# Flamingo stack on one core: layer 2's first group ahead of layer 1's last down products, and three tiles' softmax weights on two engines

## The chip, the cores and the metric

The kernel runs on one core of a Trainium2 chip as one launch. The metric is the device time of a run in microseconds (us), lower is better. A core has five engines that work side by side, each through its own queue in order: TensorE (PE in the profile, with PEld for its weight loads), VectorE (DVE), ScalarE (ACT), GpSimd (POOL) and SyncE (SP, which here only issues DMAs). Three timed runs of the kernel before took 826.50, 824.56 and 826.20 us, median 826.2 us.

## The reference, cut to what matters

The input x has 4 sequences of 256 tokens, each 256 wide: 1024 tokens. Eight steps follow each other, each adding a gated residual:

```python
x = x + tanh(g_xattn[0]) * L0_xattn(layernorm(x), ctx)   # latent attention, 16 heads, 64 context rows
x = x + tanh(g_ffn[0])   * L0_ffn(layernorm(x))          # 16 experts, top 6
x = x + tanh(g_xattn[1]) * L1_xattn(layernorm(x), ctx)   # latent attention without rope on the queries
x = x + tanh(g_ffn[1])   * L1_ffn(layernorm(x))          # ternary weights, 256 -> 1024 -> 256, gelu
x = x + tanh(g_xattn[2]) * L2_xattn(layernorm(x), ctx)   # 16 heads of 16, causal mask
x = x + tanh(g_ffn[2])   * L2_ffn(layernorm(x))          # int8 linear
x = x + tanh(g_xattn[3]) * L3_xattn(layernorm(x), ctx)
x = x + tanh(g_ffn[3])   * L3_ffn(layernorm(x))          # 8 experts, top 2
```

Each attention takes `softmax(scores)` over 64 context rows for each of 16 heads: per token 16 groups of 64 numbers, each group less its maximum, through exp, and divided by its sum. `layernorm` takes mean and variance over the 256 columns of a token. The change concerns the end of `L1_ffn` (its second product, here called the down product), the start of `L2_xattn`, and the division by the sum in `L0_xattn` and `L1_xattn`.

## The kernel before, in words

The 1024 tokens are 8 tiles of 128 (`NT = 8`), in two groups of 4 (`NG = 2`, `TPG = 4`). x stays on chip; tile t is `x[t]`, 128 x 256.

All four attentions run through `in_flight` (L519), a loop of 11 steps written out by hand. Step i does, in this order: one step of a generator `beside` (other work that is laid between); `scores(i)`: products into a PSUM tile "wide", then maximum (`mx`), subtraction and exp into the tile `attn`; `gated_add(i - 3)`, which adds the finished tile to x (L517); `weights(i - 1)` (L486); and `attend(i - 2)`. There are two buffers of "wide", so scores(i) can start only when the subtraction of tile i - 2 has read its buffer, and four PSUM buffers "mm" for nearly everything else.

`weights` (L486) adds up each of the 16 groups of 64 (L490, VectorE), inverts the sums (L491, VectorE) and multiplies the whole 128 x 1024 tile `attn` by them in place on GpSimd (L492). `attend` begins with `transposed_pairs` (L498): eight 128 x 128 transposes on TensorE (L506) in two halves of four, each half copied out by ScalarE (L507) into `attnT`. The first half reads the first 512 columns of `attn` (heads 0 to 7), the second half the rest. In layers 0 and 1 (`latent_attend`, L677) eight products follow (L714). In layers 2 and 3 (`attention23`, L1037) come eight small products (L1109), a ScalarE copy (L1118) and the output product (L1121).

`attention23` has its own `queries(g)` for a group of 4 tiles: `layernorm(g)` (statistics L430 and L433 on VectorE, a square root L435 on ScalarE, a reciprocal L438 and four normalisations L449 on VectorE), `transposed` (L461, copies L169 or L171), and `head_queries` (L1028: eight products L476, and two ScalarE multiplications L1034). Group 0 of layer 2 is made beforehand, inside `ffn1` (L1886), and handed over as `kept[2, 0]`; group 1 is the generator's first three steps, so it lies at steps 0, 1 and 2 of `in_flight`, beside steps of `keys_values` for layer 3.

`ffn1` ends with the eight down products `down(g, i)` (L1916): 24 products of 128 x 256 in bf16 (L1920), an addition of the bias (L1928) and a gated addition (L517). Between those of group 1 it lays the steps of `keys_values(2, ...)` (L987: a memset, two key products L1000 with VectorE writes L1007, and four value products L1016 with copies), `layernorm(0)`, `transposed(xn)` and `head_queries(2, ...)`. After them, `used("L1_w2")` frees a weight slot, so that the next load (`w_L_sgu`) is issued, and `load_experts3` (L325) issues the loads of four experts of layer 3, two DMAs each, into the space that held the hidden activations.

The order of instructions on each engine is set by a scheduler when the program is built: it takes what is ready by its own estimate of times, and among what is ready the earlier in the program's text. `side_by_side` (L150) raises the priority of all but the first product of the scores.

Of the kernel before, what the change touches and what calls it, by code (L numbers as in the profile page):

```python
# [97 lines left out]
def tile_flamingo(ctx: ExitStack, tc: tile.TileContext, a: dict, out: bass.AP):  # L98
# [212 lines left out]
    def used(name):  # L311

        del loaded[name]
        at[1] += 1
        issue()
# [167 lines left out]
        nc.vector.tensor_tensor(e, src, mx.unsqueeze(2).to_broadcast([P, groups, n]), ALU.subtract)  # L483
        nc.scalar.activation(e, e, AF.Exp)  # L484

    def weights(e):  # L486

        groups, n = e.shape[1], e.shape[2]
        sm = sb.tile([P, 16], F32, tag="sm", name="sm", bufs=3)[:, :groups]
        nc.vector.tensor_reduce(sm, e, AX.X, ALU.add)  # L490
        nc.vector.reciprocal(sm, sm)  # L491
        nc.gpsimd.tensor_tensor(e, e, sm.unsqueeze(2).to_broadcast([P, groups, n]), ALU.mult)  # L492

    def softmax_inplace(e, src):
        exponentials(e, src)
# [20 lines left out]
    def gated_add(t, ps, gate):  # L516
        return nc.vector.scalar_tensor_tensor(x[t], ps, gate, x[t], ALU.mult, ALU.add)  # L517

    def in_flight(scores, attend, gate, beside=iter(())):  # L519

        made, outs = {}, {}
        for i in range(NT + 3):
            next(beside, None)
            if i < NT:
                made[i] = scores(i)
            if i >= 3:
                gated_add(i - 3, outs.pop(i - 3)[:, :D], gate)
            if 1 <= i <= NT:
                weights(made[i - 1])
            if 2 <= i < NT + 2:  # L530
                outs[i - 2] = attend(i - 2, made.pop(i - 2))

# [144 lines left out]
    def latent_attend(products, wvo, gate, swapped=False, beside=iter(())):  # L677


        vos: dict = {}  # L680

        def values(b):

            v = region(("wqk", "weff")[b % 2], 2048, "vo").rearrange("p (q j o) -> p q j o", q=4, j=2)
            for r in range(2):
                pss = [ps_mm() for _ in range(2)]
                for a_ in range(2):
                    for j, ps in enumerate(pss):
                        rows = slice(j * DC, (j + 1) * DC)
                        nc.tensor.matmul(  # L690
                            ps[a_ * L : (a_ + 1) * L, :],
                            bd_k[rows, b, j * L : (j + 1) * L],
                            wvo[rows, 4 * r + a_ : 4 * r + a_ + 3 : 2, :],
                            start=True,
                            stop=True,
                        )
                for j, ps in enumerate(pss):
                    evacuate(v[:, 2 * r : 2 * r + 2, (1 - j) if swapped and b >= B // 2 else j, :], ps.rearrange("p (q o) -> p q o", q=2))
            vos[b] = v.rearrange("p q j o -> p (q j) o")

        def scores(t):
            if t % 2 == 0:
                values(t // 2)
            ps = ps_wide()
            products(ps, t)
            e = t4([P, NH, L], "attn")
            exponentials(e, ps.rearrange("p a (h l) -> p (a h) l", l=L))
            return e

        def attend(t, e):  # L710
            aT, vo = transposed_pairs(e), vos[t // 2]
            ps = ps_mm()
            for s in range(NP):
                nc.tensor.matmul(ps[:, :D], aT[:, s, :], vo[:, s, :], start=(s == 0), stop=(s == NP - 1))  # L714
            return ps

        in_flight(scores, attend, gate, beside)

    def attention0(gate):

# [316 lines left out]
    def attention23(layer, gate, beside):  # L1037
        kbd, vbd = kept.pop(layer)
        w = loaded[f"L{layer}"]
        w_o = w[:, 512:1024].rearrange("p (c o) -> p c o", c=2)  # L1040
        qT = []

        def queries(g):

            xn = layernorm(g, layer == 3)
            yield
            xT = transposed(xn)
            yield
            qT.append(head_queries(layer, xT))

        if (layer, 0) in kept:
            qT.append(kept.pop((layer, 0)))
        else:
            for _ in queries(0):
                pass

        def scores(t):


            g, i = divmod(t, TPG)  # L1060
            ps = ps_wide()
            masked = t % 2 == 0
            if masked:
                for a in range(2):
                    nc.tensor.matmul(
                        ps[:, a, :].rearrange("p (h l) -> p h l", l=L),
                        ident16,
                        causal16.unsqueeze(1).to_broadcast([P, 8, L]),
                        start=True,
                        stop=False,  # L1070
                    )

            def part(half, a):
                rows = slice(a * L, (a + 1) * L)
                return nc.tensor.matmul(
                    ps[:, a, half * D : (half + 1) * D],
                    qT[g][rows, half, i * P : (i + 1) * P],
                    kbd[rows, half, t // 2].rearrange("p i l -> p (i l)"),
                    start=not masked,
                    stop=(half == 1 or not masked),  # L1080
                )

            last = side_by_side(lambda half=half, a=a: part(half, a) for half in range(2) for a in range(2))
            if layer == 3 and t == 2:
                kept_busy(1, ps_mm(), last)

            e = t4([P, NH, L], "attn")
            src = ps.rearrange("p a (h l) -> p (a h) l", l=L)
            mx = small([P, NH], "mx")
            nc.vector.tensor_reduce(mx, src, AX.X, ALU.max)  # L1090
            for a in range(2):
                nc.vector.tensor_tensor(
                    e.rearrange("p (f a i) l -> p a f i l", f=2, a=2)[:, a],
                    ps[:, a, :].rearrange("p (f i l) -> p f i l", f=2, l=L),
                    mx[:, a * 8 : (a + 1) * 8]
                    .rearrange("p (f i) -> p f i", f=2)
                    .unsqueeze(3)
                    .to_broadcast([P, 2, 4, L]),
                    ALU.subtract,
                )  # L1100
            nc.scalar.activation(e, e, AF.Exp)
            return e

        def attend(t, e):
            aT = transposed_pairs(e)
            ps = ps_mm()
            for pr in range(NP):
                half, r = divmod(pr, 4)
                nc.tensor.matmul(  # L1109
                    ps[r * 32 : (r + 1) * 32, half * P : (half + 1) * P],  # L1110
                    vbd[:, t // 2, pr].rearrange("p j d -> p (j d)"),
                    aT[:, pr, :],
                    start=True,
                    stop=True,
                    tile_position=(0, r * 32),
                )
            cT = sb.tile([P, 2 * P], F32, tag="xn", name="ctxTok", bufs=AHEAD + 2)
            nc.scalar.copy(cT, ps[:, : 2 * P])  # L1118
            ps = ps_mm()
            for half in range(2):  # L1120
                nc.tensor.matmul(  # L1121
                    ps[:, :D], cT[:, half * P : (half + 1) * P], w_o[:, half, :], start=(half == 0), stop=(half == 1)
                )
            return ps

        in_flight(scores, attend, gate, zip_longest(queries(1), beside))
        if layer == 3:
            used("L3")

# [756 lines left out]
    def ffn1(gate):  # L1886
# [29 lines left out]
        def down(g, i, terms):  # L1916
            ps = ps_mm()
            for f in range(8):
                for k in range(3):
                    nc.tensor.matmul(  # L1920
                        ps[:, :D],
                        terms[:, k, f, i * P : (i + 1) * P],
                        w2[:, f, :],
                        start=(f == 0 and k == 0),
                        stop=(f == 7 and k == 2),
                    )
            y = sb.tile([P, D], F32, tag="xn", name="y", bufs=AHEAD + 2)
            nc.vector.tensor_tensor(y, ps[:, :D], b2_1, ALU.add)  # L1928
            gated_add(g * TPG + i, y, gate)

        terms = [up(g) for g in range(NG)]
        used("L1_w1")
        for i in range(TPG):
# [1 line left out]
        kept["values"] = values = region("wqk", 2048, "values")  # L1935
        keys = keys_values(2, region("weff", 2048, "kbd2"), values[:, :1024])
        next(keys)
        down(1, 0, terms[1])
        next(keys)
        xn = layernorm(0)  # L1940
        down(1, 1, terms[1])
        next(keys)
        down(1, 2, terms[1])
        for _ in range(2):
            next(keys)
        down(1, 3, terms[1])
        xT_2 = transposed(xn)
        for _ in keys:
            pass
        kept[2, 0] = head_queries(2, xT_2)  # L1950
        used("L1_w2")
        load_experts3(EARLY3, E3)


    def quantised():
# [240 lines left out]
```

## Time and profile before

One execution was profiled. Its own time was 824.72 us, its span (first to last instruction) 822.9 us; so 1.8 us lie around the span.

| | busy us | share of the span | instructions |
|---|---|---|---|
| PE (matmuls) | 776.0 | 94% | 4507 |
| PEld (weight loads) | 520.6 | 63% | 4510 |
| DVE | 497.2 | 60% | 1146 |
| ACT | 291.7 | 35% | 508 |
| POOL | 246.0 | 30% | 211 |

| stage | us from the span's start |
|---|---|
| layer 0 attention, its tiles in flight | 142.7 to 204 |
| layer 0 experts | 204 to 395 |
| layer 1 attention, its tiles in flight | 408 to 483 |
| layer 1 FFN | 483 to 530 |
| layer 2 attention, its tiles in flight | 535 to 584.5 |
| layer 2 FFN | 584.5 to 599 |

In a timeline a row gives start, length, engine, line, operation, output and inputs, how many such instructions the row merges, and in brackets how long the engine stood idle before it and which instruction ended that. "L492" is line 492 of the kernel.

### The profile page before, as it was taken

The numbers are of one execution on the slowest core, as the hardware profiler recorded it, in microseconds if no ns is written. First come the engines' busy times: TensorE is split into PE (matmuls) and PEld (weight loads), VectorE is DVE, ScalarE is ACT, GpSimd is POOL, SyncE is SP. The second block draws the span as 40 slices with busy tenths as digits, with TensorE's granted clock in tenths as the row PEclk, the third lists the DMA queues.
The fourth block names the chain that finished last, engine by engine and source line by source line (L and its number), as shares of the span: only waits on it lengthen the run. The fifth ranks groups of instructions, "written<-read, shape, count | busy, mean of one in ns | idle before, by whom it ended". The sixth has DMA issues, their size and how long they took to land. (4 is left out here: it accounts for less than half of the span.)

```text
span 822.9 us, 12507 instructions
## 1 busy us (share of the span) xinstructions
PE 776.0 (94%) x4507; PEld 520.6 (63%) x4510; DVE 497.2 (60%) x1146; ACT 291.7 (35%) x508; POOL 246.0 (30%) x211
## 2 busy tenths in 40 slices
PE   6999999898999999999999999998798899999994
PEld 5544433787564776766556566755445647999993
DVE  5565455874693455534878759888769564334331
ACT  3121112343421333422543568166455421233320
POOL 1355444322123344222021110024424103444332
PEclk9999999999999999999999999999999999999998
DMA  9510115800121253333930001630000102232211
GB/s 358 181 39 0 58 39 190 281 18 11 30 63 50 68 130 73 64 74 81 336 111 1 8 1 33 229 129 1 26 1 2 52 9 78 54 50 42 29 16 18
DMA packets 32467, 62.44 MB, mean 76 GB/s; under 512 B 5552, under 2 KB 19504, under 8 KB 31696
## 3 DMA queue, kind: packets, MB, share of 16 engines
q1 hardware_dynamic: 25008, 51.91, 18.3%
q0 software_dynamic: 7104, 9.41, 6.9%
q8 instruction: 39, 0.64, 0.3%
q10 hardware_dynamic: 288, 0.26, 0.1%
q14 instruction: 28, 0.23, 0.1%
HBM read 52.81 MB, written 9.27 MB: 75 GB/s over the span
## 5 line engine op out<-in xcount | busy, mean ns | idle before, releaser
L492 POOL TENSOR_TENSOR attn<-attn,sm 128x1024 f32<-128x1024 f32 x32 | 61.1, 1911 | 219.3 <-DVE sm L491 170.9
L476 PE MATMUL wide<-xT,big 128*128 128x512 f32 (+1 forms) x240 | 108.6, 600 | 1.1 <-DVE shared L1678 0.9
L742 DVE TENSOR_TENSOR rope<-wide,big 128x512 f32<-128x512 f32 x96 | 59.6, 684 | 51.9 <-PE wide L476 51.9
L476 PEld LDWEIGHTS wide<-xT,big 128*128 128x128 f32 (+1 forms) x240 | 43.4, 188 | 57.3 <-issue 49.3
L1451 PE MATMUL wide<-blk,still 128*128 128x128 f32 x640 | 74.8, 275 | 0.6 <-DVE blk L1423 0.6
L1451 PEld LDWEIGHTS wide<-blk,still 128*128 128x128 f32 x640 | 73.1, 192 | 0.8 <-issue 0.8
L714 PE MATMUL mm<-vo,attnT 128*128 128x256 f32 x256 | 58.6, 382 | 1.5 <-ACT attnT L507 1.5
L476 PE MATMUL wide<-xT,dense 128*128 128x512 f32 (+1 forms) x120 | 55.1, 598 | 0.0
L714 PEld LDWEIGHTS mm<-vo,attnT 128*128 128x128 f32 x256 | 47.8, 190 | 11.4 <-ACT attnT L507 3.3
L507 ACT COPY attnT<-mm 128x512 f32<-128x512 f32 x64 | 34.5, 587 | 43.3 <-PE mm L506 42.9
L490 DVE TENSOR_REDUCE sm<-attn 128x16 f32<-128x1024 f32 x32 | 38.7, 1209 | 15.2 <-ACT attn L484 13.8
L1413 DVE COPY still<-big 128x1024 f32 x20 | 13.9, 694 | 52.1 <-PE wide L1451 44.5
L1485 POOL DMA_INDIRECT out_dram<-ring,scratch x20 | 31.5, 1577 | 39.5 <-DVE ring L1478 15.6
L1485 POOL DMA_INDIRECT sums<-ring,big x17 | 26.8, 1575 | 48.5 <-ACT ring L1567 18.9
L1469 PE MATMUL mm<-big,hidden 128*128 x160 | 37.8, 380 | 1.4 <-DVE hidden L1462 1.4
L506 PE MATMUL mm<-ident,attn 128*128 128x128 f32 x256 | 34.6, 279 | 4.6 <-POOL attn L492 4.6
L1386 POOL DMA_INDIRECT xs<-xd,scratch x20 | 20.0, 1002 | 62.1 <-PE mm L1420 31.5
L506 PEld LDWEIGHTS mm<-ident,attn 128*128 128x128 f32 x256 | 29.9, 143 | 12.8 <-POOL attn L492 7.9
L1461 ACT ACTIVATE hidden<-wide 128x512 f32<-128x512 f32 x20 | 12.0, 598 | 71.2 <-PE wide L1451 65.7
L476 PEld LDWEIGHTS wide<-xT,dense 128*128 128x128 f32 (+1 forms) x120 | 21.5, 185 | 24.4 <-issue 22.7
L517 DVE SCALAR_TENSOR_TENSOR x<-mm,tg,x 128x256 f32<-128x256 f32 x44 | 20.4, 469 | 26.6 <-PE mm L714 15.0
L796 ACT COPY big<-mm 128x512 f32<-128x512 f32 x16 | 8.6, 589 | 67.9 <-PE mm L784 61.7
(363 smaller groups left out, 1575.8 us busy)
## 6 DMA issues: line engine op xcount, KB each, us to landing
big<-in_L_w_gate_up SPq DMA_DIRECT2D x8, 1024.0 KB, 12.0
big<-in_L_w_down SPq DMA_DIRECT2D x8, 512.0 KB, 9.0
w_L_qk<-in_L_qk SPq DMA_DIRECT2D x4, 896.0 KB, 7.3
big<-in_L_w SPq DMA_DIRECT2D x2, 1480.0 KB, 8.1
big<-in_L_w SPq DMA_DIRECT2D x2, 1110.0 KB
big<-in_L_wo SPq DMA_DIRECT2D x1, 2048.0 KB, 15.3
big<-in_L_w SPq DMA_DIRECT2D x2, 1024.0 KB, 5.3
xd<-xn SPq DMA_DIRECT2D x16, 128.0 KB, 1.9
```

The costliest lines, as they stand in the source:

```text
L476: nc.tensor.matmul(ps, w(c), xT[:, c, :], start=(c == 0), stop=(c == 1))
L490: nc.vector.tensor_reduce(sm, e, AX.X, ALU.add)
L492: nc.gpsimd.tensor_tensor(e, e, sm.unsqueeze(2).to_broadcast([P, groups, n]), ALU.mult)
L506: nc.tensor.transpose(ps[:, i * P : (i + 1) * P], ev[:, pr * P : (pr + 1) * P], ident)
L507: nc.scalar.copy(aT[:, half * 4 : half * 4 + 4, :].rearrange("p i t -> p (i t)"), ps)
L517: return nc.vector.scalar_tensor_tensor(x[t], ps, gate, x[t], ALU.mult, ALU.add)
L714: nc.tensor.matmul(ps[:, :D], aT[:, s, :], vo[:, s, :], start=(s == 0), stop=(s == NP - 1))
L742: nc.vector.tensor_tensor(m[:, s, :].rearrange("q (b t) -> q b t", t=S), ps[:, s, :].rearrange("q (b t) -> q b t", t=S), table, ALU.mult,)
L1386: nc.gpsimd.indirect_dma_start(out=xs, out_offset=None, in_=self.xd, in_offset=bass.IndirectOffsetOnAxis(ap=self.gather[:, b : b + 1].bitc ...
L1451: made = nc.tensor.matmul(ps[:, k, f : f + P], w[:, at : at + P], st[:, c * P : (c + 1) * P], start=(c == 0), stop=(c == 1),)
L1469: made = nc.tensor.matmul(ps[:, :D], hT[:, j * P : (j + 1) * P], self.w[:, bass.ds(r + j * D, D)], start=(j == 0), stop=(j == n - 1),)
L1485: nc.gpsimd.indirect_dma_start(out=self.sums[b % len(self.sums)], out_offset=bass.IndirectOffsetOnAxis(ap=self.scatter[:, b : b + 1].bitca ...
```

## The change

Two things are changed. First, `weights` gets a switch `shared`; where it is set, the multiplication is cut in two: VectorE multiplies heads 0 to 7, GpSimd heads 8 to 15. It is set for tiles 0, 6 and 7 in `latent_attend`, so in layers 0 and 1. Second, the end of `ffn1` is put in another order: `layernorm(0)` stands ahead of down(1, 0), the transposes and head queries of layer 2's group 0 stand ahead of down(1, 2), and down(1, 2), down(1, 3), the last two value products, the freeing of the slot and the experts' loads become a generator of two steps, which layer 2's `in_flight` runs at its steps 0 and 1. Layer 2's `queries(1)` thereby moves from steps 0 to 2 to steps 2 to 4. Layer 3 has nothing under `"others"`, so it stays as it was.

```diff
-    def weights(e):
+    def weights(e, shared=False):
...
-        nc.gpsimd.tensor_tensor(e, e, sm.unsqueeze(2).to_broadcast([P, groups, n]), ALU.mult)
+        parts = [(nc.vector, slice(0, groups // 2)), (nc.gpsimd, slice(groups // 2, groups))]
+        for engine, part in parts if shared else [(nc.gpsimd, slice(0, groups))]:
+            one = e[:, part]
+            engine.tensor_tensor(one, one, sm[:, part].unsqueeze(2).to_broadcast(list(one.shape)), ALU.mult)
...
-    def in_flight(scores, attend, gate, beside=iter(())):
+    def in_flight(scores, attend, gate, beside=iter(()), shared=()):
...
-                weights(made[i - 1])
+                weights(made[i - 1], shared=i - 1 in shared)
...
-        in_flight(scores, attend, gate, beside)
+        in_flight(scores, attend, gate, beside, shared=(0, NT - 2, NT - 1))
...
-        in_flight(scores, attend, gate, zip_longest(queries(1), beside))
+        in_flight(scores, attend, gate, zip_longest(chain(kept.pop("others", ()), queries(1)), beside))
...
+        def down_2():
+            down(1, 2, terms[1])
+            yield
+            down(1, 3, terms[1])
+            for _ in keys:
+                pass
+            used("L1_w2")
+            load_experts3(EARLY3, E3)
+            yield
+
...
         next(keys)
+        xn = layernorm(0)
         down(1, 0, terms[1])
         next(keys)
-        xn = layernorm(0)
         down(1, 1, terms[1])
         next(keys)
-        down(1, 2, terms[1])
+        xT_2 = transposed(xn)
         for _ in range(2):
             next(keys)
-        down(1, 3, terms[1])
-        xT_2 = transposed(xn)
-        for _ in keys:
-            pass
         kept[2, 0] = head_queries(2, xT_2)
-        used("L1_w2")
-        load_experts3(EARLY3, E3)
+        kept["others"] = down_2()
```

## The prediction

> **What bounds the kernel now.** I read the page first, for the engines' shares, then the waits of PE, then the timelines of the three stretches that the change touches, then the window table for the clock.
>
> ```profile
> PE 776.0 (94%) x4507; PEld 520.6 (63%) x4510; DVE 497.2 (60%) x1146; ACT 291.7 (35%) x508; POOL 246.0 (30%) x211
> ```
>
> PE is busy for 776.0 of 822.9 us and the change adds and removes no matmul, so at most 46.9 us of PE idling can be had anywhere, and the change can only reach what lies in its stretches. PE's timeline of layer 0's tiles:
>
> ```profile
> 150.97 0.46 PE L841 MATMUL wide<-bd_k,big 128*128 128x128 f32 x2 [0.56 <-DVE attn L483]
> 153.08 1.09 PE L506 MATMUL mm<-ident,attn 128*128 128x128 f32 x8 [1.65 <-POOL attn L492]
> ...
> 193.95 1.09 PE L506 MATMUL mm<-ident,attn 128*128 128x128 f32 x8 [0.99 <-POOL attn L492]
> 195.34 3.72 PE L714 MATMUL mm<-vo,attnT 128*128 128x256 f32 x16 [0.29 <-ACT attnT L507]
> ```
>
> The first tile's transposes wait 1.65 us for GpSimd's multiplication, the seventh's 0.99; the eighth's (198.89) wait for nothing. Layer 1, all engines:
>
> ```profile
> 419.29 0.24 DVE L491 RECIPROCAL sm<-sm 128x16 f32<-128x16 f32 x1
> 419.70 1.90 POOL L492 TENSOR_TENSOR attn<-attn,sm 128x1024 f32<-128x1024 f32 x1 [30.73 <-DVE sm L491]
> 421.66 1.09 PE L506 MATMUL mm<-ident,attn 128*128 128x128 f32 x8 [0.30 <-POOL attn L492]
> ```
>
> Only 0.30 us there; layer 1's last two tiles (transposes at 473.15 and 478.09) do not wait for GpSimd. The start of layer 2, all engines:
>
> ```profile
> 535.29 0.30 PEld L1075 LDWEIGHTS wide<-kbd,xT 64*128 64x128 f32 x4 [0.76 <-ACT xT L1034]
> 536.05 0.30 PEld L1075 LDWEIGHTS wide<-kbd,xT 64*128 64x128 f32 x4 [0.46 <-ACT xT L1034]
> 536.80 1.23 DVE L1090 TENSOR_REDUCE mx<-wide 128x16 f32<-128x1024 f32 x1 [2.27 <-PE wide L1075]
> 539.20 3.70 PE L476 MATMUL mm<-xT,w_L 128*128 128x512 f32 x8
> 540.03 1.28 ACT L1101 ACT_TABLE_LOAD   x1
> 546.04 1.09 PE L506 MATMUL mm<-ident,attn 128*128 128x128 f32 x8 [0.91 <-POOL attn L492]
> ```
>
> From the first scores' maximum to the first transposes 9.24 us pass, but PE has group 1's transposes, queries (3.70) and two more tiles' scores to do meanwhile, and idles 0.91 only. The two weight-load rows show a second thing: half of a tile is read as soon as that half is written.
>
> **Part one, two engines.** Six multiplications of 128x1024 (1.90 us) become six on VectorE and six on GpSimd of 128x512. On VectorE the nearest row is L1735, same shape, both inputs on chip: 0.68. On GpSimd L492 itself took 1.90 for 1024 columns and 0.40 for 128, so 1.67 ns a column, and 1.05 for 512 (L750, without broadcast, 1.27, is the upper end). Whether the two run beside each other:
>
> ```profile
> 572.86 1.90 POOL L492 TENSOR_TENSOR attn<-attn,sm 128x1024 f32<-128x1024 f32 x1 [3.47 <-DVE rstd L438]
> 572.98 1.80 DVE L442 SCALAR_TENSOR_TENSOR shift<-mv,rstd 128x4 f32<-128x4 f32 x1
> ```
>
> A VectorE operation on four columns, 0.16 us in its median, took 1.80 and ended with GpSimd's. So I take them one after the other. VectorE issues its half right behind the reciprocal, GpSimd 0.14 later, so VectorE goes first: its half is there 0.7 after the reciprocal, GpSimd's at 0.68 + 1.05 = 1.7, where the whole tile now takes 0.14 + 1.90 = 2.04. Side by side it would be 1.2.
>
> [...] In the other direction, GpSimd behind VectorE, the trace has only 2.21 against 1.90 at 447.53.
>
> Tile 0 of layer 0: the reciprocal ends at 150.98. The first four transposes can run from 151.7, the last four from 152.7 (0.5 us), and the scores behind them start at 153.2 instead of 154.01: -0.8. VectorE is full there (3.89 and 4.00 busy of the 4.00 us windows from 152), so its 0.68 delays tile 1's sum; GpSimd then ends tile 1 at 158.4, where PE will want it at 158.2. Net -0.6; bounds -1.3 (side by side) and +0.2 (only waiting moves). PE then has no wait until 188, so this arrives at the tail. Tile 6: four transposes start when PE is free (192.96), the rest at 193.6 instead of 193.95, and the first copy is out at 194.3, so L714 starts then instead of at 195.34: -1.0; bounds -1.28 (both waits gone) and -0.3 (all eight wait for the second half). Tile 7: 0, it has 2.4 us to spare. Layer 1: tile 0 -0.3, tiles 6 and 7 0 (the 0.68 falls into VectorE's gaps at 467 and 475). Sum **-1.9**, bounds -2.9 and -0.4.
>
> **Part two, the order around layer 2.** Moved behind: 48 down products (2 x 2.79 us), two bias and two gated additions (0.42 and 0.48 each), two value steps (1.13 on PE, four copies), nine DMA issues (eight of the experts, one of `w_L_sgu`). SP waits in these now (530.30) and has nothing behind them until 584.50; what they load is read after 650. Landing 12 us, 6 us later: 0, and all of their cover, over 100 us, would have to go before it cost anything.
>
> PE from the end of the second key products (523.2): transposes 1.04, four value products 1.13, queries 3.70, down(1, 2) 2.79, scores 1.13: 533.0, where the first scores now end at 536.76. Normalised tokens are there in time (523.08 now, and they move up). Then down(1, 3) 2.79, values 1.13, two key products of 0.70, scores 1.13 and 1.74: PE is full to 541.2. Tile 0's chain of 9.24 less the copy that lay in it (0.68) gives transposes at 541.7, against 546.04: -4.3. But the next tile's maximum and subtraction may step between sum and reciprocal, as in layer 0's tile 6 (sum 187.82, reciprocal 191.61): +2.5, transposes at 544.2, of which PE can fill 1.8 with a key step and the fourth scores. Group 1's transposes and queries (1.04 + 3.70 = 4.74), until now done while PE had to wait anyway, come afterwards, into a stretch in which PE idles some 1.2 us from 546 to 567 (0.49 twice, 0.29 before L1121 and smaller ones) and VectorE hardly at all (4.00 of 4.00 from 552 to 564); group 1's layernorm adds 4.0 us there (0.6 a tile twice, the normalisations 1.4, the rest earlier in its gaps). So early: -4.3 + 4.74 - 1.2 = -0.8; late: -1.8 + 4.74 - 1.2 - 1.8 = -0.1. I take the middle, **-0.5**. VectorE runs a tile ahead (recip of tile 4 at 559.91, its transposes at 567.14), so its 4 us are hidden by that lead of 5; without it they would cost up to 4.
>
> New waits: L435's square root now comes between exponentials, so ScalarE loads its tables twice more (2 x 1.28 + 0.30 = 2.87). Behind it stand the exponential of tile 1 or 2 and the `attnT` copies. From 538 to 544 nobody waits for ScalarE: 0; bound +2.87. Four more tiles' worth of later scores may also fill the gaps of the tail (6 us idle from 567 to 584.5): bound -2.5 for part two.
>
> The clock: in the tail PE idled 0.98 of the microsecond from 572, and then
>
> ```profile
> 575.00:576.00 1.00, 1.00 (x4) 0.63 (x3) 0.00 (x0) 0.00 (x0) 0.00 (x0) 0.50 0.00 0
> ```
>
> half clock for some 3.5 us: L1121 took 1.76 instead of 1.13, L506 1.91 instead of 1.04, together 1.5 us. It is the square root of L435 that causes it (table load at 570.86), which stays; I leave it at 0, bounds -1.5 and +1.5. [...]
>
> **Sum.** -1.9 - 0.5 = -2.4 against the profiled execution: span 820.5, with the 1.8 us around it 822.3. That execution (824.72) lies 1.5 below the median of the three runs (826.2), so on the median's scale 826.2 - 2.4 = **823.8 us**.
>
> **Rivals.** (A) The halves exclude each other and nothing else moves: all eight transposes wait for the second half (-0.3 in layer 0's tile 6, 0 to -0.3 in the first tiles), part two is an exchange of equal work: -1.0, **825.2**. For: the 1.80 us row; VectorE full at 152. Against: the half-wise reads at 535.29 and 536.05. (B) More: late scores spread into the tail (part two -2.5), the tail's clock holds (-1.5 in part), with part one -1.9: -5, **821**. For: 6 us idle in the tail; against: VectorE, full from 552, does not let the scores drift far. (C) Slower: ScalarE's tables in layer 2. The square root of group 1 falls among the exponentials and copies with PE waiting: +2.87, nothing absorbed and transposes at 544.2 (-1.8 + 4.74): together +5.8, less 1.9: +3.9, **830**. It decides from the point where the square root comes later than the first transposes (542 to 544); at 570.86 the same load already stops PE by 1.03 us. Against: statistics of all tiles are ready by 538.
>
> **Chances.** Forecast 0.38, A 0.29, B 0.18, C 0.15. A measurement of this kernel can tell 0.3%, 2.5 us, from no change, so the border is 823.7, and the forecast case lies on it: 0.21 of it faster, 0.17 same. A gives 0.27 same and 0.01 on each side, B 0.18 faster, C 0.13 slower and 0.02 same. Faster 0.40, same 0.46, slower 0.14. The range takes in B down to 820.0 and C up to 828.5.
>
> **What would show it.** In layer 0 the transposes of tiles 0 and 6 split into two rows of four, tile 6's L714 a microsecond earlier; GpSimd's half starts beside VectorE's but ends 1.7 us after the reciprocal, not 1.2. In layer 2 the first maximum some 3.8 us earlier against its own down products, a table load of L435 between two of L1101, and the transposes from tile 4 on at nearly the old times. I am wrong if PE waits for `attnT` or `xT` before 565, or if the gaps of the tail are filled.

## The result, and the profile after

The changed kernel took 829.72 us (median of 13 runs, 827.10 to 832.92) against 826.37 us for the kernel before in the same measurement (13 runs, 824.56 to 829.12): a ratio of 1.0040, interval 1.0027 to 1.0053. It is slower by 0.4%, where I had predicted 823.8 us and a range of 820.0 to 828.5. The profiled execution took 831.03 us, its span is 829.2 us. The engines' shares of the changed kernel's page:

```profile
PE 778.1 (94%) x4507; PEld 522.8 (63%) x4510; DVE 501.2 (60%) x1152; ACT 294.7 (36%) x510; POOL 242.1 (29%) x211
```

PE does the same work (776.0 before). What the span grew by, 6.3 us, is idling and half clock, part of it in stretches that the change does not touch: PE's first wait for `w_L_qk` (1.44 us, none before) and a dip of the clock in layer 0's experts (granted 0.50 from 271 to 273, 1.00 before) together put the changed execution 3.3 us behind. So I compare stretches between two fixed rows instead of times from the start. Behind layer 2's stretch both profiled executions take the same 238.5 us: the moved loads delay nothing. The changed `weights` is 3 lines longer, so the lines behind it are numbered 3 higher (more in runs with further edits): L492 is now L495, L506 L509, L507 L510, L517 L520, L714 L717, L1075 L1078, L1090 L1093, L1101 L1104, L1109 L1112, L1121 L1124.

**Layer 0's tile 6**, all engines (start, length, engine, line; in brackets the idle time before and what ended it):

```profile
193.75 0.24 DVE L491 RECIPROCAL sm<-sm 128x16 f32<-128x16 f32 x1
193.91 0.37 DVE L430 BATCH_NORM_STATS2 st<-x 128x6 f32<-128x256 f32 x1
194.13 1.04 POOL L495 TENSOR_TENSOR attn<-attn,sm 128x512 f32<-128x512 f32 x1 [8.57 <-DVE sm L491]
194.19 1.53 DVE L495 TENSOR_TENSOR attn<-attn,sm 128x512 f32<-128x512 f32 x1
...
195.78 1.09 PE L509 MATMUL mm<-ident,attn 128*128 128x128 f32 x8 [0.67 <-DVE attn L495]
```

A VectorE instruction (L430) has slipped in behind the reciprocal, so GpSimd starts first, and VectorE's half, 0.69 us where it starts first (197.24, tile 7's), takes 1.53 and ends 0.55 behind GpSimd's. It is the half that the first four transposes need. PE's wait falls from 0.99 to 0.67. From the third tile's transposes to the end of layer 0's attention the time shrinks by 0.31 us, and that is all that layer 0 gives.

**Layer 1's last tiles**, all engines, before and then after:

```profile
472.58 0.25 DVE L491 RECIPROCAL sm<-sm 128x16 f32<-128x16 f32 x1
472.75 0.39 DVE L517 SCALAR_TENSOR_TENSOR x<-mm,tg,x 128x256 f32<-128x256 f32 x1
...
473.15 1.04 PE L506 MATMUL mm<-ident,attn 128*128 128x128 f32 x8
```

```profile
469.44 1.54 DVE L495 TENSOR_TENSOR attn<-attn,sm 128x512 f32<-128x512 f32 x1
...
475.67 0.60 PE L509 MATMUL mm<-ident,attn 128*128 128x128 f32 x4
475.94 0.25 DVE L491 RECIPROCAL sm<-sm 128x16 f32<-128x16 f32 x1
476.23 0.69 DVE L495 TENSOR_TENSOR attn<-attn,sm 128x512 f32<-128x512 f32 x1
476.84 0.48 DVE L520 SCALAR_TENSOR_TENSOR x<-mm,tg,x 128x256 f32<-128x256 f32 x1
477.46 0.63 PE L509 MATMUL mm<-ident,attn 128*128 128x128 f32 x4 [1.20 <-DVE x L520]
```

The gated addition (L520) empties the PSUM buffer that the second four transposes of tile 6 write to: they wait for it. Before, it stood right behind tile 7's reciprocal; now a half of tile 7 stands between, and a half of tile 6, which took 1.54 us behind the start of GpSimd's (469.39), has pushed the whole chain back. PE waits 1.20 us for it, where it waited for nothing.

**Layer 2's start**, all engines:

```profile
542.75 1.28 ACT L435 ACT_TABLE_LOAD   x1
...
544.22 0.24 DVE L491 RECIPROCAL sm<-sm 128x16 f32<-128x16 f32 x1
544.63 1.90 POOL L495 TENSOR_TENSOR attn<-attn,sm 128x1024 f32<-128x1024 f32 x1 [65.03 <-DVE sm L491]
...
546.59 1.92 PE L509 MATMUL mm<-ident,attn 128*128 128x128 f32 x8 [2.62 <-POOL attn L495]
...
556.44 0.91 PE L1112 MATMUL mm<-attnT,values 128*32 128x128 f32 x16 [1.03 <-ACT attnT L510]
558.81 3.60 PE L476 MATMUL mm<-xT,w_L 128*128 128x512 f32 x8
563.95 1.23 DVE L1093 TENSOR_REDUCE mx<-wide 128x16 f32<-128x1024 f32 x1 [3.77 <-PE wide L1078]
```

PE waits 2.62 us for the first weights, against 0.91 before. Behind the wait its clock is at half (L509 takes 1.92, not 1.09). Group 1's queries (L476) follow only at 558.81, and while PE makes them VectorE stands idle for 3.77 us. The windows show the clock (columns: window, its length, busy time of PE, PEld, DVE, ACT and POOL, granted clock, DMA share, GB/s):

```profile
545.00:546.00 1.00, 0.00 (x0) 0.00 (x0) 1.00 (x4) 0.98 (x4) 1.00 (x1) 1.00 0.87 336
547.00:548.00 1.00, 1.00 (x7) 1.00 (x6) 1.00 (x4) 0.99 (x2) 0.00 (x0) 0.50 1.05 430
```

Two yardsticks are used from here. **Layer 1's end**: from the start of its tile 5's transposes to the first key products of layer 2 (L1000): 51.86 us before (467.39 to 519.25), 53.29 after. **Layer 2's stretch**: from that row to the end of its last output products: 65.22 before, 67.53 after; "lost" is the stretch's time weighted by one minus the granted clock. Half clock for 3.41 us shows as a loss of 1.7 us, and "at full clock" is said of a stretch without such a fall. Taking the loss off a stretch gives an estimate, and rather too low a one: one fall in the old order's tail lengthened the stretch by 1.07 to 1.57 us (64.92 to 65.42 in four traces, against 63.85).

| kernel | layer 2's stretch | lost to half clock | first transposes after its start | third tile's |
|---|---|---|---|---|
| before | 65.22 | 1.71 | 26.79 | 37.81 |
| after | 67.53 | 1.70 | 23.40 | 40.64 |
| order alone | 68.97 | 3.40 | 23.40 | 42.07 |
| ... five matmuls in the wait | 67.52 | 0 | 25.10 | 40.63 |
| ... three matmuls in the wait | 66.79 | 0 | 23.39 | 39.90 |
| ... no square root | 69.03 | 3.42 | 23.40 | 42.14 |
| ... first tile not normalised | 67.99 | 3.42 | 20.71 | 41.16 |
| ... half moved | 73.41 | 6.82 | 29.52 | 46.50 |
| old order: engines alone | 65.42 | 1.71 | 26.80 | 37.81 |
| old order: without layer 1's tail | 63.85 | 0 | 26.79 | 37.81 |
| new order, one group's queries | 62.07 | 1.71 | 23.40 | 36.45 |
| old order, one group's queries | 66.06 | 3.42 | 27.71 | 39.70 |

### The profile page after: what moved, and what is told of

It is laid out like the page before. It is cut to its first block, busy times and chain, and to the rows that moved or that the text cites. A ratio compares the mean times of both kernels' runs of the same rounds, so it can differ in the third digit from the quotient of the medians.

```text
span 829.2 us, 12521 instructions
## 1 busy us (share of the span) xinstructions
PE 778.1 (94%) x4507; PEld 522.8 (63%) x4510; DVE 501.2 (60%) x1152; ACT 294.7 (36%) x510; POOL 242.1 (29%) x211
## 5 line engine op out<-in xcount | busy, mean ns | idle before, releaser
L495 POOL TENSOR_TENSOR attn<-attn,sm 128x1024 f32<-128x1024 f32 (+1 forms) x32 | 57.2, 1790 | 232.0 <-DVE sm L491 170.8
L476 PE MATMUL wide<-xT,big 128*128 128x512 f32 (+1 forms) x240 | 108.6, 600 | 1.1 <-DVE shared L1681 0.9
L476 PEld LDWEIGHTS wide<-xT,big 128*128 128x128 f32 (+1 forms) x240 | 43.4, 188 | 57.3 <-issue 49.3
L717 PE MATMUL mm<-vo,attnT 128*128 128x256 f32 x256 | 58.6, 382 | 1.6 <-ACT attnT L510 1.2
L476 PE MATMUL wide<-xT,dense 128*128 128x512 f32 (+1 forms) x120 | 55.1, 599 | 0.0
L717 PEld LDWEIGHTS mm<-vo,attnT 128*128 128x128 f32 x256 | 47.8, 190 | 11.5 <-issue 3.0
L510 ACT COPY attnT<-mm 128x512 f32<-128x512 f32 x64 | 34.5, 587 | 38.2 <-PE mm L509 37.8
L509 PE MATMUL mm<-ident,attn 128*128 128x128 f32 x256 | 34.9, 279 | 6.8 <-POOL attn L495 3.9
L509 PEld LDWEIGHTS mm<-ident,attn 128*128 128x128 f32 x256 | 29.7, 143 | 15.2 <-POOL attn L495 5.9
L476 PEld LDWEIGHTS wide<-xT,dense 128*128 128x128 f32 (+1 forms) x120 | 21.5, 185 | 24.4 <-issue 22.1
L520 DVE SCALAR_TENSOR_TENSOR x<-mm,tg,x 128x256 f32<-128x256 f32 x44 | 20.6, 472 | 26.2 <-PE mm L717 12.7
```

What stands on the lines that cost most here:

```text
L476: nc.tensor.matmul(ps, w(c), xT[:, c, :], start=(c == 0), stop=(c == 1))
L495: engine.tensor_tensor(one, one, sm[:, part].unsqueeze(2).to_broadcast(list(one.shape)), ALU.mult)
L509: nc.tensor.transpose(ps[:, i * P : (i + 1) * P], ev[:, pr * P : (pr + 1) * P], ident)
L510: nc.scalar.copy(aT[:, half * 4 : half * 4 + 4, :].rearrange("p i t -> p (i t)"), ps)
```

## The experiments

Times are medians. Ratios are to the kernel before, with a 95% interval; they come from all runs and need not be the quotient of the two medians. "The same" below is within 0.3%.

### The two parts, each alone

`e1_order_alone` has the new end of `ffn1` and of `in_flight`'s generator, and no `shared`; `e2_engines_alone` has `shared` and the old order.

> The order of layer 2 alone, every multiplication of the weights on GpSimd as before. Theory 1 (most of the loss is the order: PE waits some 2.6 us for layer 2's first weights, and its clock falls behind that wait, 1.8 us; in the changed kernel's trace layer 2's stretch lost 2.3): 2.3 us over before, 1 to 4, since the clock's part may differ from run to run. Rival (the order costs nothing; all comes from layer 1's last tiles, where VectorE's halves stand ahead of the gated additions): within 0.5 us of before.

> Two engines in layers 0 and 1, tiles 0, 6 and 7, with the old order of layer 2. Theory 1, by the offsets of the two traces: -0.3 in layer 0, -0.5 at layer 1's tile 0, +1.4 at layer 1's end: 0.7 us over before. The prediction's own part one: 1.9 under before. Rival (the two engines cost nothing but gain nothing): within 0.3.

Measured: the order alone 829.27 against 825.83 us, ratio 1.0035 (1.0018 to 1.0052); the engines alone 826.96, ratio 1.0011 (0.9997 to 1.0025). So the order makes most of the loss, 2.9 us by its ratio, and the two engines lose 0.9 instead of gaining 1.9. The interval of the second just includes no change, but its stretch at layer 1's end is 53.29, the same 1.43 longer as in the changed kernel.

### Where the two engines lose

```diff
-        in_flight(scores, attend, gate, beside, shared=(0, NT - 2, NT - 1))
+        in_flight(scores, attend, gate, beside, shared=(0, NT - 2, NT - 1) if swapped else (0,))      # e3
+        in_flight(scores, attend, gate, beside, shared=() if swapped else (NT - 2, NT - 1))           # e4
+        in_flight(scores, attend, gate, beside, shared=() if swapped else (NT - 2,))                  # e9
+        in_flight(scores, attend, gate, beside, shared=() if swapped else (NT - 1,))                  # e10
```

`swapped` holds in layer 0 only.

> As two engines alone, but layer 1 shares only tile 0; layer 0 still shares 0, 6 and 7. Theory 1: 0.8 us under before (-0.3 and -0.5), 1.4 under two engines alone. Rival (layer 1's last two tiles cost nothing, the offset of 1.4 was noise): the same as two engines alone.

> Only layer 1's tiles 6 and 7 are shared, nothing else is changed. Theory 1: 1.4 us over before, through the gated additions that come behind VectorE's halves, with PE waiting for x at the transposes of tile 6 and 7. Rival (VectorE's gaps take the halves up, as predicted): 0.

Measured: without layer 1's tail 824.73 us, ratio 0.9990 (0.9974 to 1.0005); the tail alone 826.53, ratio 1.0007 (0.9993 to 1.0021). The totals point the right way but do not decide; the stretch does: 51.85 without the tail, 53.30 with the tail alone (469.29 to 522.59). Then each tile by itself:

> Only layer 1's tile 6 is shared between two engines, nothing else is changed; read in the stretch from layer 1's sixth transposes (tile 5) to layer 2's first key products, 51.86 us before, 53.29 with tiles 6 and 7 shared. Theory (each VectorE half delays the gated addition that empties the PSUM buffer of the next transposes: tile 6's by 0.89, since it is held until GpSimd ends and pushes the next maximum back, tile 7's by 0.68; some 0.35 of it was slack): 0.5 longer, 52.4. Rival (only tile 7's half, which stands directly ahead of the gated addition, counts): 51.9.

> Only layer 1's tile 7 is shared; the same stretch. Theory: 0.68 less 0.35 of slack, 52.2. Rival (tile 7's half alone makes the whole loss): 53.3.

One run each, 824.96 and 826.45 us; the stretches are 52.68 (468.05 to 520.73) and 52.44 (468.35 to 520.79): +0.82 and +0.58, together 1.40 of the 1.43. PE's rows, tile 6 shared and then tile 7:

```profile
474.80 0.63 PE L509 MATMUL mm<-ident,attn 128*128 128x128 f32 x4 [0.38 <-DVE x L520]
```

```profile
474.97 0.66 PE L509 MATMUL mm<-ident,attn 128*128 128x128 f32 x4 [0.26 <-DVE x L520]
```

In both the wait is for the gated addition. I had allowed for 0.35 us of slack in each and there was hardly any: nearly all of each half's delay (0.89 and 0.68) arrives.

### The halves exchanged

```diff
-        parts = [(nc.vector, slice(0, groups // 2)), (nc.gpsimd, slice(groups // 2, groups))]
+        parts = [(nc.gpsimd, slice(0, groups // 2)), (nc.vector, slice(groups // 2, groups))]
```

on top of the kernel without layer 1's tail.

> As two engines without layer 1's tail, with the halves exchanged: GpSimd multiplies heads 0 to 7, which the first four transposes need, VectorE heads 8 to 15. Theory (in layer 0 GpSimd starts first and VectorE is held until it ends, so the half that is needed first comes last): the first four transposes of layer 0's tiles 0 and 6 come some 0.5 us earlier each, 1.0 in all, so 2.1 us under before. Rival (both halves are needed before anything follows, or VectorE goes first once it has the other half): the same as without the exchange, 1.1 under before.

Measured: 825.55 us, ratio 0.9989 (0.9974 to 1.0004), no different from the 0.9990 without the exchange. The trace explains half of the miss. Layer 0's tile 6, PE:

```profile
190.94 3.72 PE L717 MATMUL mm<-vo,attnT 128*128 128x256 f32 x16 [0.29 <-ACT attnT L510]
194.78 1.27 PE L509 MATMUL mm<-ident,attn 128*128 128x128 f32 x8
```

The transposes start 3.84 us after the products ahead of them, 4.41 without the exchange (191.60 to 196.01) and 4.71 before (189.24 to 193.95), and they wait for nothing: 0.57 won, as expected. Tile 0's transposes come 0.65 earlier too (3.87 after L841's row, 4.52 without the exchange), but the third tile's then stand where they stood before, 19.15 to 19.17 after that row in all three kernels: at the second tile PE now waits 0.26 us for GpSimd, 0.49 without the exchange and 0 before. That VectorE, which is full there, takes the gain back is likely but was not tested. So 0.57 of the expected 1.0 is in the trace, and the total cannot show so little.

### Layer 2: tables, clock, first wait

All of these start from the order alone.

```diff
+    def layernorm(g, scalar=False, after=(), func=AF.Sqrt):                                    # e7
+        made = nc.scalar.activation(rstd, mv[:, :, 1], func, bias=eps)
+            xn = layernorm(g, layer == 3, func=AF.Identity if layer == 2 and g == 1 else AF.Sqrt)
...
+            if layer == 2 and t == 2:                                                          # e6; e11 with 3
+                kept_busy(5, ps_mm(), last, "L2")
...
-            if 1 <= i <= NT:                                                                   # e13, bare=(0,) in layer 2
+            if 1 <= i <= NT and i - 1 not in bare:
                 weights(made[i - 1])
```

> As the order alone, but ScalarE's square root for layer 2's second group of tokens is replaced by an identity with the same bias, of the same shape: the table loads go, and the second group's tokens are scaled by another factor, so the square root is left out. Rival C of the prediction (the tables are the price): the exponentials and attnT copies behind come 1.3 to 2.9 us earlier and the time falls by as much against the order alone. Theory (PE waits for VectorE's sums and reciprocal and for GpSimd; ScalarE's loads lie beside that): first transposes at the same place after layer 2's first scores (10.9 us), time within 0.7 us of the order alone.

Its stretch is 69.03 against 68.97, the first transposes at the same 23.40, although ScalarE is busy 2.5 us less in it (34.17 against 36.65). The tables are not the price. (Its total, 857.38 us, says nothing: the values of layer 3 are others.)

> As the order alone, with five matmuls of 128x512 without use (about 0.46 us each, 2.3 in all) behind the third tile's scores of layer 2, in the 2.6 us in which PE waits for the first weights. Theory (the idle 2.6 us let the clock fall to half behind the first transposes, 1.8 us, and the wait itself stays): 1.8 us under the order alone, so some 1.6 over before; the rows of the first transposes and of the scores behind them are back at 1.09 and 1.13. Rival 1 (the clock isn't the price, or it then falls at the next gap): the same as the order alone, 3.4 over before. Rival 2 (the matmuls hold up what follows): more than that.

> As the order alone, with three matmuls without use in place of five: five took 4.56 us (0.91 each) and so ended 1.7 us after the first weights were there; three take 2.7 and end with the wait. Layer 2's stretch, from its first key products to the end of its last output products, was 65.2 us before, 69.0 with the order alone, 67.5 with five. Theory (of the 3.8 of the order alone some 3.4 are half clock, and the five held the clock but came 1.7 too late): the stretch falls to 65.8 and the time to within 1 us of before. Rival (the clock only hides other idling: what PE doesn't lose to it, it then waits for ScalarE and VectorE): 67.5 again, some 2 to 4 over before.

Five matmuls: 829.88 us, ratio 1.0048 (1.0030 to 1.0065); three: 828.84, ratio 1.0043 (1.0028 to 1.0058). The order alone had 1.0035. By the totals, nothing was won. By the traces the half clock is gone in both; with three, PE reads:

```profile
542.44 2.84 PE L515 MATMUL mm<-w_L,ident 128*128 128x512 f32 x6
545.13 1.09 PE L509 MATMUL mm<-ident,attn 128*128 128x128 f32 x8
...
552.35 1.09 PE L509 MATMUL mm<-ident,attn 128*128 128x128 f32 x8 [0.47 <-POOL attn L495]
554.25 0.92 PE L1114 MATMUL mm<-attnT,values 128*32 128x128 f32 x16 [0.81 <-ACT attnT L510]
```

The stretch comes to 66.79, between the 65.8 of my theory and the 67.5 of the rival: of 3.4 us lost to the clock in the order alone 2.2 came back, the rest turned into waits for GpSimd, ScalarE and VectorE. The old order's stretch at full clock is 63.85, so at full clock on both sides the new order still loses 66.79 - 63.85 = 2.94 us. My theory that the clock was most of the loss fell here. The runs say the same: the median of their mean granted clocks is 0.993 for the kernel before, 0.990 with the order alone and 0.993 again with three matmuls, and yet the time is no shorter (1.0043 against 1.0035).

> As the order alone, but layer 2's first tile leaves out its sum, reciprocal and multiplication (its weights aren't normalised), so its transposes wait for the exponential only. Read layer 2's stretch alone (what lies behind it depends on the values). Theory 1 (PE's wait of 2.6 us for the first weights, with the half clock behind it, makes the loss): the wait goes, no half clock before 555, the stretch comes to 65 or less. Rival (the loss is the second group's 4.74 us of transposes and queries, which now stand in the middle of the layer): the wait goes but PE waits as long further back, 67 to 69.

The first wait is gone (first transposes at 20.71), and the stretch is still 67.99: PE now waits 2.22 us for VectorE a tile later, and a fall of the clock of twice the length (6.83 us) comes with it. Without that (lost: 3.42) the stretch would be some 64.6. So the 67 to 69 of the rival is met only through the clock, and the 65 or less of theory 1 would be met without it: this run does not decide between the two. It shows that taking one wait away hands it on.

### The second group's queries

`e8_half_moved` leaves down(1, 2) ahead of the queries and moves only down(1, 3).

> As the order alone, but only the last down product, the last two key steps and the loads behind them are put behind the first scores; the last but one stays ahead of the queries, and the second group's transposes and queries are issued one tile earlier. Theory (what costs is that the second group's 4.74 us no longer lie in PE's wait for the first weights): they come again before or beside that wait, PE's wait is under 1 us and the clock holds; within 1 us of before. Rival (any down product between the first scores and the first weights delays VectorE's sum and costs the same): 3.4 over before.

Measured 834.87 us, ratio 1.0102 (1.0080 to 1.0124): both expectations missed by far. The second group's normalisations and transposes now fall between the first tile's maximum and its sum, on a VectorE with one gap of 0.20 us there. The first exponential ends at 545.33, its sum starts at 548.02, the first transposes come 29.52 after the stretch's start. The clock falls twice, for 3.41 and for 10.24 us, 6.82 us lost in all; without that some 66.6 remain. So this run tests neither expectation: it makes a new delay of its own.

The last pair leaves PE's work for the second group out, and the copies behind it, in either order:

```diff
+            if layer == 2 and g == 1:
+                yield
+                qT.append(qT[0])
+                return
             xT = transposed(xn)
             yield
             qT.append(head_queries(layer, xT))
```

> The order alone, with PE's work for layer 2's second group left out (8 transposes 1.04, 8 query products 3.60 to 3.70, their four copies on ScalarE and VectorE): the second group's tiles take the first group's queries; its normalisation stays. Read layer 2's stretch only, at full clock 66.8 in the new order (69.0 with half clock in two places), and the third tile's transposes, 39.9 to 42.1 after its start. Theory (in the new order this work stands in PE's way while VectorE idles 3.8 us, in the old it lies in PE's wait for the first weights): 4 to 5 shorter, 62 to 63 at full clock. Rival (the work costs the same at both places, and the loss is the waits for VectorE and ScalarE): as much shorter as the old order without it.

> The kernel before with the same work left out. Its stretch was 63.9 at full clock, 65.3 with the half clock in the tail. Theory: PE waits that much longer for the first weights, whose transposes stay within 1 us of 26.8 after the stretch's start; stretch within 1 us of 63.9 or 65.3. Rival: 4 to 5 shorter, 59 to 60 at full clock, as in the new order.

PE's waits up to the first transposes, and its last output products (L1128 and L1125 here), in the new order (start of the stretch 523.14) and in the old (520.76):

```profile
546.54 1.09 PE L509 MATMUL mm<-ident,attn 128*128 128x128 f32 x8 [2.63 <-POOL attn L495]
...
584.08 1.13 PE L1128 MATMUL mm<-w_L,ctxTok 128*128 128x256 f32 x4 [0.55 <-ACT ctxTok L1125]
```

```profile
540.93 0.60 PE L1069 MATMUL wide<-causal,ident 128*128 128x512 bf16 x2 [0.93 <-DVE attn L1096]
...
543.47 1.13 PE L1079 MATMUL wide<-kbd,xT 64*128 64x256 f32 x8 [0.87 <-DVE attn L1096]
546.94 1.03 PE L1069 MATMUL wide<-causal,ident 128*128 128x512 bf16 x2 [2.34 <-DVE attn L1096]
548.47 1.97 PE L506 MATMUL mm<-ident,attn 128*128 128x128 f32 x8 [0.49 <-POOL attn L492]
...
585.69 1.13 PE L1125 MATMUL mm<-w_L,ctxTok 128*128 128x256 f32 x4 [0.55 <-ACT ctxTok L1122]
```

The new order's stretch falls to 62.07 us, 5.5 less than the changed kernel's with the same one fall of the clock; without the fall some 60.4, even less than the 62 to 63 that I expected. The old order's stretch does not shrink: 66.06 with a fall of twice the length, within 1 us of 65.3 as expected, and some 62.6 without it, against 63.9. PE only waits in the work's place, 0.93, 0.87, 2.34 and 0.49 us, 4.63 in all, where it waited 0.91. The same work, 4.7 us of PE and four copies, is worth 5.5 us where the change puts it and 0 to 1.2 where it was. And without this work the new order is the shorter of the two, by some 2 to 4 us: what makes layer 2 longer is where the change puts the second group's queries. (What lies behind layer 2 depends on the values, so the totals, 851.82 and 852.46, say nothing.)

### A version meant to beat both

`e16_old_order_three_edits`: the old order; layer 0's tile 6 with the halves exchanged, layer 1's tile 0 as in the change, nothing else shared; and in layer 2

```diff
             aT = transposed_pairs(e)
+            if layer == 2 and t == 5:
+                kept_busy(1, ps_mm(), kept["turned"], "L2")
```

> The old order with what the runs spoke for: layer 0's tile 6 shared with GpSimd on the first half (0.86 by its trace), layer 1's tile 0 shared as in the change (0.46), and in layer 2 one matmul of 128x512 without use (0.91) behind the sixth tile's transposes, in the 1.0 us in which PE waits for ScalarE and behind which the clock fell to half in four of seven traces of this order (1.0 to 1.5 us each). Theory: 2 us under before, the stretch of layer 2 at 63.9 with full clock. Rival (the matmul delays what follows, or the clock falls elsewhere): 1 under, or none.

Measured 823.54 against 826.04 us, ratio 0.9987 (0.9968 to 1.0005): faster than the changed kernel, but not to be told from the kernel before; by its ratio 1.1 us under it, where the rival had 1. Its trace has full clock through the tail and a stretch of 63.87. That the matmul did this is not shown, since three of the seven traces without it have no fall there either.

```profile
571.61 1.02 PE L517 MATMUL mm<-w_L,ident 128*128 128x512 f32 x2
572.81 0.91 PE L1116 MATMUL mm<-attnT,values 128*32 128x128 f32 x16 [0.17 <-ACT attnT L512]
```

## Why the prediction was wrong

**The step that failed** is in part two, the overlap of the moved work: "Group 1's transposes and queries (1.04 + 3.70 = 4.74) ... come afterwards, into a stretch in which PE idles some 1.2 us", with VectorE's share "hidden by that lead of 5". That this work had lain in a wait I knew; its price in the new place I had wrong. I priced the gain, the earlier first transposes, at -4.3, or at -1.8 with another 1.8 of the wait filled. It is -3.4, and nothing was filled: PE idles for all of the 2.62 us, and the fourth scores come behind the transposes (548.44). I priced the return at +4.74 less 1.2, so +3.54, and it is +6.3. Nothing of the work was hidden, and it drew more behind it: from the first to the third tile's transposes the old order needs 11.0 us, the new one at full clock 16.5 (39.90 - 23.39), so 5.5 more, of which 4.64 are the work; the rest comes with new waits, the 0.47 and 0.81 among them. From the third tile's transposes to the end it needs 0.85 more again (26.89 against 26.04). VectorE's lead of a tile is gone: it stands idle for 3.77 us in front of the fifth tile, whose scores need these queries. Without the work that wait is gone (up to the fifth tile's maximum VectorE then waits 0.70 us at most), and the part from the third tile on takes 25.62. Together -3.4 + 5.5 + 0.85 = +2.95, where the sum had -0.5; the bound of +2.87 was for ScalarE's tables, which cost nothing. The pair of runs without this work shows it directly: nearly free in PE's old wait, 5.5 us in its new place. The old wait of 0.91 was short because that very work filled it: without the work it is 4.63.

**The clock.** I left it at 0. The new wait of 2.62 us was followed by a fall in all four traces of the new order that have it; the old order's tail had one in four of seven traces that keep layer 2 as it was. In the profiled pair both kernels lose 1.7 us, and it about cancels. Holding it in the new order saved 2.2 us of one trace and nothing that a total shows.

**Part one, layer 1's end: 0 predicted, +1.43 measured**, settled by the runs of tiles 6 and 7 alone. "The 0.68 falls into VectorE's gaps" was true of VectorE and wrong of the path: behind the half stood the gated addition, and behind that a PSUM buffer that PE needed. I named who waits for GpSimd and not who waits for VectorE.

**Part one, layer 0: -1.6 predicted, -0.31 measured.** That one half is to be counted after the other held in every row: the half that starts second takes longer, VectorE's 1.27 to 1.54 us instead of 0.69, GpSimd's 1.45 to 1.48 instead of 1.04. That "VectorE goes first" did not hold in the two tiles that were to gain, 0 and 6: a copy or a statistics row stood between, GpSimd started 0.05 to 0.31 us earlier and VectorE's half came last. Exchanging the halves moved tile 6's transposes by another 0.57, which shows the cause. Tile 0's gain does not arrive at the third tile in any version, against "PE then has no wait until 188". Layer 1's tile 0: -0.3 predicted, -0.46 by the trace (reciprocal to transposes 1.91 instead of 2.37).

**The signs I had asked for.** The table load of L435 between two exponentials: there. The first maximum 3.8 us earlier against its own down products: 3.4 earlier in the stretch (14.18 after its start instead of 17.55). Transposes from tile 4 on at nearly the old times: no, 4.4 later. Two rows of four in layer 0: no. "Wrong if PE waits for `attnT` before 565": it does, 1.03 at 556.44.

**Rival C** gave 830, which is the right time in good part by luck. Its "nothing absorbed" (-1.8 + 4.74 = +2.94) is what layer 2 shows, though from other terms. Its +2.87 for the tables did not come: without their loads the stretch is 69.03 instead of 68.97. That error is made up by part one, which it took at -1.9 and which is +0.66.

**The sum now**: -0.31 and -0.46 for the two gains, +1.43 for layer 1's end, +2.94 for layer 2, together +3.6 us at full clock, or +3.0 with the 2.31 of the profiled pair for layer 2; measured +3.3 (2.2 to 4.4 by the interval). What stays open is the clock's share in the totals: the runs that hold it differ by less than their intervals.

## What to carry to other kernels

Before work is moved out of a wait, price the wait as it will be without it: a short wait may be short because that work lies in it. Leaving the work out in both orders, one run each, tells what it costs at each place. An operation that is given to another engine is to be priced by who is queued behind it and what they set free (here a PSUM buffer), and where the half that starts second ends late, as here (VectorE's took 1.53 us behind GpSimd's, 0.69 ahead of it), the half that is needed first belongs to the engine that will start first.

## What the runs showed of the hardware

A fall of PE's clock to half (0.50 granted) lasted 3.41 us, with 1.70 or 1.71 us lost, or a whole multiple of that (6.83 and 10.24 us). It followed PE's wait of 2.62 or 2.63 us in all four traces that have it, 0.09 to 1.61 us behind the wait's end, and the one of 1.03 or 1.04 in layer 2's tail in four of the seven traces of the old order, 1.54 to 2.29 us behind. Why three of the seven have none is not shown. Where a trace has two falls in or behind layer 2's stretch, they start 20.48 us apart (before: 574.72 and 595.20), 54.62 (after: 546.68 and 601.30), 10.25 (order alone), 10.24 (no square root) and 6.82 (half moved), each within 0.02 us of a whole multiple of 3.413. How long PE was busy just ahead does not tell a fall by itself: in the kernel before it was busy for 1.82 of the 3.41 us ahead of the fall at 574.73, and for 1.81 of the 3.41 us from 151.48, with a granted clock of 1.00 behind them.

The two halves of a tile overlap in time, and the one that started second took longer. Where GpSimd started first (layer 0's tiles 0 and 6, layer 1's tile 6), its half took 1.04 us and VectorE's 1.27, 1.53 and 1.54, ending 0.54 or 0.55 behind it. Where VectorE started first (layer 0's tile 7, layer 1's tiles 0 and 7), its half took 0.69 and GpSimd's 1.45 to 1.48, ending 0.90 or 0.91 behind it.
